# Queuing the ranking of a block's tokens in its last chunk's fifth turn instead of after its ninth

## The chip, the cores and the metric

The kernel runs on one core of one Trainium2 chip. The metric is the device time of one execution in microseconds (us). Before the change it is 3864.69 us, the median of four runs that lie between 3862.81 and 3876.28 us.

## The reference, cut to what matters

The program computes two layers, each of two halves. The change lies in the last quarter: a recurrence over 512 time steps, whose output goes token by token through a mixture of experts.

```python
def step(h_prev, xw_t):                       # second recurrence, 512 steps, batch 8, width 256
    h_next = jnp.tanh(xw_t + h_prev @ Wh)
...
router_logits = jax.nn.sigmoid(x @ gate_w + gate_b)             # 16 experts
expert_values, expert_indices = jax.lax.top_k(router_logits, k=2)
expert_values = expert_values / jnp.sum(expert_values, axis=-1, keepdims=True)
...
expert_weighted = jnp.sum(expert_values[..., None] * selected, axis=2)
return x + _mlp(x, shared_wg, shared_wu, shared_wd) + expert_weighted
...
x = x + _L1_ffn_ref(_L1_cond2_ref(x, cond_1024, ...), ...)      # experts of the recurrence's output
```

The tokens that enter the experts are the recurrence's hidden states; `_mlp` is the shared expert.

## The kernel before, in words

Everything up to the second recurrence (attention, a first recurrence, routed heads, adapters, a second attention) takes the first 3.1 ms and is not touched. `rnn_moe` (printed below) then runs the recurrence and the experts side by side on one core.

**Steps and passes.** The main loop makes 512 passes, one for each time step t. A pass issues, in this order: the step itself (`rnn_step`: 16 small matmuls of L1538 into `pg`, one tanh on ScalarE at L1540, one transpose on VectorE at L1541 that writes `ring`, which the next step's matmuls read); what an earlier pass left for later (`consume`); one piece of ranking (`ranks`); one piece of collecting (`gathers`); and one piece of bulk work, from `chunks` if there is one, else from `big`. A pass with neither gets one filling matmul (L1958). PE, ScalarE and VectorE execute in exactly this written order. POOL and SP are ordered by the scheduler.

**Chunks and blocks.** 16 steps (128 tokens) make a chunk. 32 chunks are cut into blocks of 9, 9, 9 and 5. When a chunk's 16 steps are done, `Experts.chunk` is queued. It takes nine turns, one in each of the following passes:

- turn 1: POOL copies the hidden states into `hT` (L1582); turn 2: nothing
- turn 3: router matmuls (L1594, L1595); their bias, sigmoid and the copy `hr` are left for the next pass
- turn 4: half of the shared expert (L1609); the maxima and their indices (`top`, `topi`, L1612, L1613) are left for the next pass
- turn 5: the other half (L1618); the gate `a` (L1622 to L1624) is left for the next pass
- turns 6 and 7: nothing; turns 8 and 9: `pd` (L1631, L1635), and the sum `acc` (L1639) left for the next pass

A turn that does nothing passes the place on to `big`.

**Ranks.** When a block's last chunk is through, `ranked(x)` is queued. `Experts.rank` turns the chosen experts into a row number for each token in a list that is sorted by expert and padded to tiles of 128 rows. That is 13 turns of small VectorE operations (L1653 to L1710) with three matmuls `pk` (L1677 to L1679) in the fifth turn. Then POOL scatters the rows of `hr` into DRAM with indirect DMAs (L1720), two for each chunk, in three turns for each pair. Each waits for the transpose of the step beside which it is issued (`paced`). Six idle turns follow, then the block's tiles are appended to `big`.

**Tiles.** A block has 33 tiles of 128 rows (25 in the last). `big` is a list worked off from the front, so the tiles of a block begin when those of the block before are done. The first five turns only load; then each tile takes three turns: two with `gate` (L1771) and a turn of the next rows (`turn`, L1761), one with `down` (L1787). POOL copies each tile's expert weights out of SBUF (L1751, L1752, two instructions) into one of four buffers, after the `down` that last used it. Outputs go to DRAM (L1792).

**Collecting.** When a block's tiles are done, POOL gathers their rows back with indirect DMAs (L1830), two for each chunk, and VectorE adds them (L1838).

After step 511 the same loop goes on without steps until all queues are empty. This part is called the drain here. It begins with the nine turns of the last chunk.

Of the kernel before, what the change touches and what calls it, by code (L numbers as in the profile page):

```python
# [1486 lines left out]
def rnn_project(K, M):  # L1487

    ahead = [chunk_x(K, M, n, "xp") for n in (1, 2)]
    for n in range(1, S // XB):  # L1490
        xc = ahead.pop(0)
        if n + 2 < S // XB:
            ahead.append(chunk_x(K, M, n + 2, "xp"))
        for m in range((n - 1) * 2 * M.NT // (S // XB - 1), n * 2 * M.NT // (S // XB - 1)):
            K.nc.sync.dma_start(out=M.xs[m // M.NT][m % M.NT * P : (m % M.NT + 1) * P, :], in_=M.zero)
        px = (M.psx, M.pxt)[n % 2].tile([P, D], F32, name="px", tag=("px", "xt")[n % 2])
        for k in range(2):
            K.nc.tensor.matmul(px, xc[:, k], M.wx[:, k, :], start=(k == 0), stop=(k == 1))
            if k == 1:
                M.later(lambda n=n, px=px: K.nc.vector.tensor_tensor(M.xw[:, n - 1, :], px, M.rbias, ALU.add))  # L1500
            yield 1


def expert_weights(K, M):

    src = M.experts.rearrange("(e p) n -> p e n", p=P)
    for e in range(16):
        K.nc.sync.dma_start(out=M.wgu[:, e], in_=src[:, e, 0 : 2 * D])
        K.nc.sync.dma_start(out=M.wdn[:, e], in_=src[:, e, 2 * D : 3 * D])
        yield 0  # L1510
# [335 lines left out]
def rnn_moe(K, out, start):  # L1846
# [3 lines left out]
    with ExitStack() as es:  # L1850
# [76 lines left out]
        big, ranks, chunks, gathers = [rnn_project(K, M), expert_weights(K, M)], [], [], []  # L1927

        def ranked(x):
            yield from x.rank()  # L1930
            for _ in range(6):
                yield 0
            big.append(tiled(x))

        def tiled(x):
            yield from x.tiles()
            gathers.append(x.collect())

        def chunk(x, c, ring):
            yield from x.chunk(c, ring)  # L1940
            if c == x.C - 1:
                ranks.append(ranked(x))

        M.left = True
        nb, at = -1, 0
        with K.tc.manual_schedule(engines={E.PE, E.Activation, E.DVE}):
            for t in range(S):
                if t % XB == 0:
                    if t == XB * sum(BLOCKS[: nb + 1]):
                        nb += 1  # L1950
                        block, at = Experts(K, M, nb), 0
                rnn_step(K, M, t)
                consume()
                advance(ranks)
                advance(gathers)
                idle = not (advance(chunks) or advance(big))
                if idle:
                    mm(M.pgu.tile([P, P], F32, name="fill", tag="gu"), K.ident, M.wx[:, 0, 0:P], start=True, stop=True)  # L1958
                for j in ((0, 1), (2,), (3,), ())[t % 4]:
                    if t // 4 * 4 + 4 < S:  # L1960
                        rnn_seed(K, M, t // 4 * 4 + 4, j)
                if t % XB == XB - 1:
                    chunks.append(chunk(block, at, M.ring))
                    at += 1
            while chunks or ranks or big or gathers:
                consume()
                M.left = bool(chunks or ranks or big)
                advance(ranks)
                advance(gathers)
                if advance(chunks) or advance(big):  # L1970
                    M.pace = M.last
            consume()
# [179 lines left out]
```

## Time and profile before

| what | us |
|---|---|
| median of four runs (3862.81, 3863.55, 3865.82, 3876.28) | 3864.69 |
| the profiled execution | 3875.72 |
| its span, first to last instruction | 3874.0 |
| first and last transpose of the recurrence (L1541, 512 of them) | 3099.5 and 3719.7 |
| the drain, from there to the end of the span | 154.3 |
| first VectorE instruction of the four ranks (L1653) | 3266.6, 3442.5, 3630.0, 3724.8 |
| scatters of the four blocks, first and last start (L1720) | 3281.3 to 3321.2, 3458.6 to 3498.0, 3646.1 to 3687.1, 3735.2 to 3757.3 |
| gathers of the four blocks, first and last start (L1830) | 3518.8 to 3597.4, 3721.6 to 3772.7, 3804.6 to 3841.4, 3855.0 to 3866.4 |

All times in the lower rows count from the span's start. The profiled execution is at the slow end of the four runs. In profile lines PE is the matmul engine, PEld its weight loads, DVE is VectorE, ACT is ScalarE, SPq is the queue of the engine that issues plain DMAs; a line ends with the idle time ahead of the instruction and what ended it.

### The profile page before, as it was taken

What the parts mean: (1) busy time and instruction counts of PE and PEld (TensorE: products, weight loads), DVE (VectorE), ACT (ScalarE), POOL (GpSimd) and SP (SyncE); (2) the same over time, 40 slices, a digit from 0 to 9 for tenths busy, and PEclk for the clock granted to TensorE, in tenths of its full rate; (3) what the DMA queues carried; (4) which work ended last, traced back from release to release, by engine and by line L of the source; (5) the groups of instructions that cost most, each with busy time, mean ns of one, the idle gap of its engine ahead of it and who ended that gap; (6) DMA issues with size and microseconds to landing.
All of it is one profiled execution on the core that took longest, in us unless ns stands there. A gap on an engine that the chain in (4) does not pass through costs nothing.

```text
span 3874.0 us, 146239 instructions
## 1 busy us (share of the span) xinstructions
PE 3442.5 (89%) x62442; PEld 2311.2 (60%) x62442; DVE 2373.8 (61%) x8871; ACT 1618.0 (42%) x5695; POOL 663.2 (17%) x1479
## 2 busy tenths in 40 slices
PE   8999888878888888699999999999999899999986
PEld 5533455555556556466656666666666666666665
DVE  4488667767777677466767666666766533243444
ACT  3111255555555555355644444444444322233333
POOL 1000000000000000000023223222323111233366
PEclk9899999999999999899999999999999999899998
DMA  3022100000000000200000000000000060122245
GB/s 111 27 83 69 32 21 16 22 21 16 5 5 5 5 4 10 75 26 26 1 3 2 1 1 2 1 2 2 1 7 1 6 210 18 59 74 81 86 128 158
DMA packets 102924, 137.91 MB, mean 36 GB/s; under 512 B 12336, under 2 KB 84048, under 8 KB 102144
## 3 DMA queue, kind: packets, MB, share of 16 engines
q1 hardware_dynamic: 88416, 89.03, 7.4%
q0 software_dynamic: 11040, 34.29, 2.7%
q8 instruction: 490, 8.03, 0.9%
q10 hardware_dynamic: 2816, 5.24, 0.4%
q14 instruction: 162, 1.33, 0.1%
HBM read 86.44 MB, written 43.25 MB: 33 GB/s over the span
## 4 chain that ended last, share of the span: by engine, by line
PE 65%; ACT 14%; DVE 12%; issue 5%; POOL 2%; DMA 1%; ACTq 0%; SPq 0%; POOLq 0%; DVEq 0%
PE pgf L678 5%; PE pg L1538 5%; PE pe L1245 4%; PE pt L1288 3%; PE po L1303 3%; DVE G L684 3%; PE pp L1205 3%; PE U L489 3%; PE pk L468 3%; PE px L1324 3%; PE pg L1771 3%; ACT th L694 3%; ACT so L685 2%; ACT left L685 2%; ACT right L685 2%
## 5 line engine op out<-in xcount | busy, mean ns | idle before, releaser
L678 PE MATMUL pgf<-wh,ring 128*16 128x64 f32 x8176 | 215.2, 223 | 201.9 <-DVE ring L695 199.5
L1541 DVE STREAM_TRANSPOSE ring<-h 128x64 f32<-128x64 f32 x512 | 125.6, 245 | 393.3 <-ACT h L1540 380.3
L678 PEld LDWEIGHTS pgf<-wh,ring 128*16 128x16 f32 x8176 | 127.4, 99 | 393.5 <-DVE ring L695 393.3
L1265 ACT ACTIVATE sm<-sm,nm 128x388 f32<-128x388 f32 (+3 forms) x512 | 283.5, 555 | 182.9 <-DVE nm L1261 182.6
L685 ACT ACTIVATE sf<-G 128x16 f32<-128x16 f32 x512 | 110.4, 216 | 462.8 <-DVE G L684 462.8
L1540 ACT ACTIVATE h<-pg 128x64 f32<-128x64 f32 x512 | 114.8, 224 | 448.9 <-PE pg L1538 397.1
L1538 PE MATMUL pg<-down,ring 128*16 128x64 f32 x8176 | 234.2, 226 | 36.6 <-DVE ring L1541 29.1
L1290 ACT COPY eT<-pt 128x512 f32<-128x512 f32 (+1 forms) x192 | 105.6, 550 | 357.0 <-PE pt L1288 356.7
L1205 PE MATMUL pp<-hn,wqkv 128*128 128x512 f32 x512 | 241.4, 615 | 0.8 <-DVE xT L932 0.8
L1288 PE MATMUL pt<-ident,sm 128*128 128x128 f32 x1280 | 192.6, 283 | 55.5 <-DVE sm L1271 41.5
L1272 POOL COPY pme<-sm 128x4 f32<-128x4 f32 x512 | 119.8, 235 | 645.3 <-DVE sm L1271 641.4
L1288 PEld LDWEIGHTS pt<-ident,sm 128*128 128x128 f32 x1280 | 148.2, 143 | 137.4 <-issue 81.7
L678 PE MATMUL pgo<-wh,ring 128*16 128x64 f32 x8176 | 216.5, 219 | 14.4 <-issue 14.0
L678 PE MATMUL pgg<-wh,ring 128*16 128x64 f32 x8176 | 212.5, 219 | 4.7 <-issue 4.4
L684 DVE STREAM_TRANSPOSE G<-pgf 128x64 f32<-128x64 f32 x512 | 127.6, 249 | 137.5 <-PE pgf L678 131.8
L637 POOL COPY xc<-xT 128x128 f32<-128x128 f32 x64 | 17.1, 296 | 1136.8 <-DVE xT L552 1025.2
L678 PE MATMUL pgi<-wh,ring 128*16 128x64 f32 x8176 | 209.6, 219 | 1.3 <-issue 1.3
L1538 PEld LDWEIGHTS pg<-down,ring 128*16 128x16 f32 x8176 | 144.9, 100 | 88.1 <-DVE ring L1541 67.5
L1261 DVE CUSTOM_DVE_ANT_0 sm<-pe,mask 128x260 f32<-128x260 f32 (+2 forms) x384 | 141.8, 425 | 89.1 <-PE pe L1245 88.9
L1771 PE MATMUL pg<-xT,w 128*128 128x128 f32 x992 | 168.6, 297 | 22.5 <-POOL w L1751 16.4
L1271 DVE TENSOR_SCALAR sm<-sm,rc 128x388 f32<-128x388 f32 (+3 forms) x512 | 176.1, 387 | 9.1
L695 DVE TENSOR_TENSOR ring<-so,th 128x16 f32<-128x16 f32 x512 | 90.0, 176 | 147.3 <-ACT th L694 147.3
(534 smaller groups left out, 8230.6 us busy)
## 6 DMA issues: line engine op xcount, KB each, us to landing
cb<-order POOLq DMA_DIRECT2D x32, 512.0 KB
x<-xs SPq DMA_DIRECT2D x124, 128.0 KB
ys<-y SPq DMA_DIRECT2D x124, 128.0 KB
xs<-zero SPq DMA_DIRECT2D x66, 128.0 KB
w<-in_ada_w_dram SPq DMA_DIRECT2D x16, 512.0 KB
w<-in_moh_w_dram SPq DMA_DIRECT2D x32, 195.0 KB
xres<-xp SPq DMA_DIRECT2D x32, 128.0 KB
xc<-xres SPq DMA_DIRECT2D x32, 128.0 KB
```

What stands on the lines that cost most here:

```text
L678: mm(dst[32 * j : 32 * j + B * (now + 1)], hp, w, start=False, stop=(k == 1), skip_group_check=True)
L684: nc.vector.transpose(G.rearrange("p k b -> p (k b)"), banks[n][0])
L685: nc.scalar.activation(to, G[:, :, B * now : B * now + B], f)
L1205: mm(pp, T.wqkv[:, k, 0 : 2048].rearrange("p (i g h n) -> p i g h n", i=2, g=4, h=2)[:, i, g, h], self.hn[b][:, k, :], start=(k == 0), sto ...
L1245: mm(pe[a][:, 0 : w - lo], q[r, h, at], k[r, h, lo:w], start=(h == 0), stop=(h == 1))
L1261: nc.vector.tensor_tensor_reduce(out=sm[a][:, lo:w], in0=pe[a][:, 0 : w - lo], in1=T.mask[:, S - n + lo : 4 + S], scale=-1.0 / 8.0, scalar ...
L1265: nc.scalar.activation(sm[a][:, 0:w], sm[a][:, 0:w], AF.Exp, bias=nm[:, a : a + 1], scale=-1.0, accum_out=su[:, a : a + 1])
L1271: nc.vector.tensor_scalar(sm[a][:, 0:w], sm[a][:, 0:w], rc[:, a : a + 1], None, ALU.mult)
L1288: nc.tensor.transpose(pt[:, at, :], sm[i * m + a][:, 4 + j * P : 4 + (j + 1) * P], K.ident)
L1538: mm(pg[32 * j : 32 * j + B * (now + 1)], hp, M.wh[:, k, 64 * j : 64 * j + 64], start=False, stop=(k == 1), skip_group_check=True)
L1541: M.pace = nc.vector.transpose(M.ring[:, B + 64 * at : B + 64 * at + 64], h)
L1771: mm(pg, W[m][:, k * D + g * P : k * D + (g + 1) * P], X[m][:, k, :], start=(k == 0), stop=(k == 1))
```

## The change

`ranked(x)` of a block is queued inside the last chunk's fifth turn, not after its ninth. The maxima and indices that the ranking reads are issued in that same pass, by its `consume`; the ranking's first piece follows in the next pass. Nothing else is edited.

```diff
         def chunk(x, c, ring):
-            yield from x.chunk(c, ring)
-            if c == x.C - 1:
-                ranks.append(ranked(x))
+            for n, used in enumerate(x.chunk(c, ring)):
+                if n == 4 and c == x.C - 1:
+                    ranks.append(ranked(x))
+                yield used
```

`rank` itself begins with `ti` copied from `topi` (L1653), and needs of the last chunk only `topi`, `top` and `hr`, all of which exist after its fourth turn.

## The prediction

> **What bounds the kernel now.** The page's busy line and its chain by engine come first: PE is busy for 89% of the span and carries 65% of the chain that ended last; POOL looks idle.
>
> ```profile
> PE 3442.5 (89%) x62442; PEld 2311.2 (60%) x62442; DVE 2373.8 (61%) x8871; ACT 1618.0 (42%) x5695; POOL 663.2 (17%) x1479
> ...
> PE 65%; ACT 14%; DVE 12%; issue 5%; POOL 2%; DMA 1%; ACTq 0%; SPq 0%; POOLq 0%; DVEq 0%
> ```
>
> That is an average over stages. The change touches only 3260 us to the end, so I read the view of waits for 3100 to 3700 us: who waited for whom, total us, times, longest.
>
> ```profile
> DVE ring L1541 <- ACT h L1540: 366.6, 454, 2.1
> ACT h L1540 <- PE pg L1538: 363.6, 438, 2.3
> POOL w L1751 <- PE py L1787: 154.4, 51, 12.1
> ```
>
> The recurrence is a ring of PE, ACT and DVE, each waiting for the one before: 512 transposes from 3099.5 to 3719.7, 620.2 us, 1.21 us a step. Its 512 steps must run whatever is queued beside them. Their pace from the timeline: steps 209 to 297 (tiles beside them, no indirect DMA) take 98.95/88 = 1.124 us each, the last three (fills beside them) 1.05. So what matters is (a) how long single steps are, (b) what work is left for the drain after step 511, which takes 3874.0 - 3719.7 = 154.3 us.
>
> **What the change moves.** The ranking is queued in the chunk's fifth turn, so its first piece falls in the sixth pass of the next chunk's time instead of the eleventh: five passes earlier. Before, the first DVE instruction of three ranks (L1653) starts at 3266.6, 3442.5 and 3630.0 us, which by counting transposes is beside steps 154, 298 and 442. They become 149, 293, 437. No instruction is added or removed; VectorE's some 30 small operations, the three `pk` matmuls and the scatters keep their number.
>
> *How far that carries* is counted from the code, pass by pass. Thirteen turns of ranking lead to the first scatter (step 167, as the trace has it: 3281.3 us), 26 more passes to the last, then idle turns.
>
> - Block 0: tiles are appended in pass 200, now 195. A chunk holds the place in its turns 3 to 5, 8 and 9, so tiles begin in pass 201, now 197: four earlier.
> - Blocks 1 and 2 do not wait for their ranks. Block 1's tiles are ready in pass 344 but the place is free in 353; block 2's in 488 but free in 510. The place becomes free when block 0's 107 turns have found room between chunks; its run starts four passes earlier but meets one chunk more, so it ends in 351, and block 1's in 508. Gain for block 2: **two passes**, not five.
> - The last block's rank starts five turns earlier in the drain, but its tiles wait for block 2's, some 60 turns later. Nothing.
>
> *What two passes are worth.* Block 2's first five turns only load. Before, they fall in passes 510 to 513 and 517, partly beside the last chunk; now in 508 to 512. Passes with nothing for PE are filled: 91 fills in the recurrence before, 91 after (two fewer ahead of block 0's tiles, five at block 1's start both ways, four instead of two at the end). In the drain 185 passes carry PE work before and 185 after; only empty passes, which issue nothing, fall from 31 to 29. So PE's work on either side of step 511 is the same, and two passes x 1.05 us = 2.1 us is not simply saved: they turn into two more fills.
>
> *The recurrence.* What makes steps long beside the ranks is the scatters. In block 2's, steps 455 to 482 take 3645.54 to 3687.26 = 41.7 us for 27 steps; at 1.125 that were 30.4; 18 scatters cost 11.3, **0.63 us each**. The timeline shows one:
>
> ```profile
> 3459.42 0.24 DVE L1541 STREAM_TRANSPOSE ring<-h 128x64 f32<-128x64 f32 x1 [0.94 <-ACT h L1540]
> ...
> 3459.72 0.42 PE L1538 MATMUL pg<-down,ring 128*16 128x64 f32 x16
> ...
> 3459.95 0.97 POOL L1720 DMA_INDIRECT xs<-hr,row  x1 [0.41 <-DVE ring L1541]
> ...
> 3461.51 0.23 ACT L1540 ACTIVATE h<-pg 128x64 f32<-128x64 f32 x1 [2.12 <-PE pt L1761]
> ...
> 3461.77 0.24 DVE L1541 STREAM_TRANSPOSE ring<-h 128x64 f32<-128x64 f32 x1 [2.10 <-ACT h L1540]
> ```
>
> PE's matmuls end at 3460.14, yet ACT starts at 3461.51, 0.6 us after the indirect DMA's issue ends: this step takes 2.35 us. The Trainium skill (SBUF — State Buffer, "SBUF: two separate sides") says that of the engines only VectorE and GpSimd contend, and PE and ACT wait for nobody; by that rule no scatter would cost anything here. The trace speaks against it, and I go by the row.
>
> All 54 scatters and 18 gathers of blocks 0 to 2 stay beside steps, five passes earlier: 0 change, between -1.9 and +1.9 if three meet steps differently (3 x 0.63). On POOL's queue they pass one chunk's `hT` copy per block (one behind them in place of two), and the idle list of PE for the stage shows no wait of L1594 on `hT`; worth nothing. The ranks' DVE work now shares passes with the chunk's gate `a` (two operations of 0.29 us) instead of a tile's `ea` (0.25 to 0.29): +0.3 at most in each of three blocks, against `pk` waits of the same size. I take 0. On SP the loads of `x` move with the tiles; L1761 waits for no DMA in this stage, so nothing is lost there.
>
> *The start of the drain.* Here an order changes. Before, POOL has the last chunk's `hT` first, then block 1's gathers; now two gathers stand ahead of `hT`.
>
> ```profile
> 3719.98 0.73 POOL L1582 COPY hT<-ring 128x128 f32<-128x128 f32 x2 [1.01 <-DVE ring L1541]
> 3720.43 0.51 PE L1594 MATMUL ph<-wr,hT 128*128 128x144 f32 x2 [0.66 <-POOL hT L1582]
> 3721.61 1.00 POOL L1830 DMA_INDIRECT yg<-ys,row  x1 [0.90 <-issue]
> 3722.91 0.97 POOL L1830 DMA_INDIRECT yg<-ys,row  x1 [0.30 <-issue]
> 3723.27 0.67 PE L1631 MATMUL pd<-wd,a 128*128 128x256 f32 x2 [0.89 <-DVE a L1624]
> ...
> 3729.15 0.61 POOL L1751 COPY w<-xT 128x512 f32 x1 [1.47 <-PE py L1787]
> ```
>
> The first gather waits for the last store of block 1's outputs (landed 3718.87 + 1.51 = 3720.38 in the chain of waits), which now comes two steps, 2.1 us, sooner: near step 510. The second is paced by step 511. Term by term:
>
> - one gather now beside a step: +0.6 (the 0.63 above; bounds 0 and 1.05, the excess of single slow steps in the gather stage)
> - `hT` behind a gather: +1.0 (bounds 0 and 2 x 1.28, the spacing of the gathers above). Queued behind `ph` on PE is all of the drain.
> - two transposes of block 2's first tile now stand ahead of `ph`: -0.4 (0.38 us, L1761)
> - PE's 0.89 wait for the gate is covered by `turn` and `gate` work that now stands ahead of `pd`: -0.9
> - the last rank's `pk` stands three gates earlier and may wait for its DVE chain: +0.4 (0.3 in the trace before; bounds 0 and 1)
> - the gathers done early free POOL, but it then waits longer for `down` (the 1.47 above): 0. After that POOL is the bound to 3758 us, with the same number of copies, scatters and gathers ahead of its ninth copy, less waits of 0.54 and 0.22: -0.8
>
> Sum: +0.6 + 1.0 - 0.4 - 0.9 + 0.4 - 0.8 = **-0.1 us**. On the profiled execution's own 3875.72 that is 3875.6. That execution lies 11.0 above the median of the four runs, so I carry the difference over: 3864.69 - 0.1, **3864.6 us**.
>
> **Clock.** The table by stretch shows granted clocks of 0.88 and 0.85 at block 0's scatters:
>
> ```profile
> 3250.00:3300.00 50.00, 46.19 (x835) 31.90 (x828) 18.60 (x88) 10.48 (x47) 14.05 (x22) 0.88 0.09 29
> 3300.00:3350.00 50.00, 44.17 (x766) 30.22 (x766) 12.64 (x59) 11.27 (x51) 11.20 (x14) 0.85 0.17 54
> ```
>
> Price: block 0's scatter steps take 42.6 us where 27 x 1.05 + 18 x 0.63 = 39.7 is due (+2.9), and the 14 steps after them 17.7 for 15.0 (+2.7): **5.6 us** for the pair of dips. The skill (TensorE: Matmul & The Clock Gate, "What's actually happening") says that the gate watches free-running windows of 3413 ns and halves the clock after an idle one; by it, dips would follow the windows' phase and not the edit, and the four runs' spread of 13.5 us would be the same after.
>
> **Rivals.**
>
> 1. *The two passes are kept and POOL is the bound from the drain's start*: -2.1 and two gathers off its queue, -2 x 1.28, gives -4.7: 3860.0. For it: POOL is saturated from 3735. Against: its 1.47 wait for PE just before.
> 2. *Five passes are gained*, as if tiles waited for ranks: -5 x 1.05 = -5.3: 3859.4. Against: the slack of 9 and 22 passes in blocks 1 and 2.
> 3. *The `hT` order decides* (slower): POOL's two gathers both go ahead, `hT` is 2.6 late, one step is 1.05 longer, and nothing covers it: +3.6: 3868.3. It decides once `hT` is later than the 1.3 us that two transposes and the gate wait cover. With one more pair of clock dips, at the four fills and the wait that now end the recurrence, +9.2: 3873.9; past 3876.3 only with a second pair.
> 4. *A pair of dips goes*: -5.6: 3859.1, with rival 1 3854.4.
>
> **How the numbers follow.** Forecast 60% (3861 to 3868); rival 1 10%, rival 2 5%, rival 3 12% (5 of them with dips), rival 4 5%, further off on the slow side 5, on the fast side 3. What a measurement of this kernel tells from no change is about 0.3%, 11.6 us: under 3853.1 faster, over 3876.3 slower. Faster 0.05 (3 far off, 2 of rival 4), slower 0.08 (5 far off, 3 of rival 3 with a second pair of dips), same 0.87. The range runs from rival 4 with 1 to rival 3 with dips: 3854 to 3874.
>
> **What would show it.** L1653 beside steps 149, 293, 437. Block 2's first transposes after step 511, as before; fills beside steps 508 to 511. The recurrence 620 +- 4 us, the drain 154 +- 3. Scatters still some 0.6 us each. Two gathers ahead of the last `hT`. I am wrong if the drain is over 4 us shorter or a stage of scatters is over 5 us longer than before at full clock.

## The result, and the profile after

The changed kernel takes 3876.56 us (median of 46 runs, 3866.14 to 3883.45). The kernel before, run in turn with it on the same chip, takes 3869.53 us (73 runs, 3860.29 to 3884.91). The ratio is 1.0018, 95% interval 1.0014 to 1.0023: **slower by 7.0 us**. That is inside the 0.3% that the prediction called no change, but it is no accident of the measurement, and the forecast of -0.1 us with its place in the middle of the range was wrong. The four runs shown before were a low sample (3864.69 against 3869.53). Laid on them, +7.0 would give 3871.7, inside the range; measured, the time lies above it.

The page's busy line and chain by engine, after the change, tell nothing of it:

```profile
PE 3440.4 (89%) x62442; PEld 2311.1 (60%) x62442; DVE 2373.6 (61%) x8871; ACT 1616.8 (42%) x5695; POOL 661.3 (17%) x1479
...
PE 65%; ACT 14%; DVE 12%; issue 5%; POOL 2%; DMA 1%; ACTq 0%; SPq 0%; POOLq 0%; DVEq 0%
```

The same holds for the view of waits for 3100 to 3700 us after the change (who waited for whom, total us, times, longest):

```profile
ACT h L1540 <- PE pg L1538: 380.0, 435, 21.4
DVE ring L1541 <- ACT h L1540: 364.6, 460, 2.9
POOL w L1751 <- PE py L1787: 155.0, 55, 8.7
```

They are the same three waits as before, of about the same size, and the longest of 21.4 us is that of the first step for work ahead of the recurrence, whose start differs from one execution to the next: its first transpose starts at 3104.26 us where it was 3099.46, though nothing before it was edited. So I compare stages from their own starts only.

| stage, us | before | after |
|---|---|---|
| profiled execution, its span | 3875.72, 3874.0 | 3877.89, 3876.1 |
| recurrence, first to last transpose (L1541) | 620.21 | 617.33 |
| steps 149 to 209 / 293 to 353 | 81.26 / 79.24 | 79.36 / 81.54 |
| steps 353 to 437 / 437 to 511 | 108.08 / 95.60 | 104.15 / 95.83 |
| drain, last transpose to end | 154.28 | 154.54 |
| last `hT` copies (L1582), after the last transpose | +0.3 | +2.9 |
| last router matmul (L1594), after it | +0.8 | +3.4 |
| first `down` of the drain (L1787), after it | +8.7 | +11.1 |

In this pair of profiles the recurrence is not slower. At the start of the drain everything is 2.4 to 2.6 us late. POOL's timeline of the changed kernel there (start, duration, operation, in brackets the idle time before it and what ended it):

```profile
3722.21 1.00 POOL L1830 DMA_INDIRECT yg<-ys,row  x1 [3.37 <-DVE ring L1541]
3723.51 0.97 POOL L1830 DMA_INDIRECT yg<-ys,row  x1 [0.30 <-issue]
3724.50 0.72 POOL L1582 COPY hT<-ring 128x128 f32<-128x128 f32 x2
...
3733.45 0.61 POOL L1751 COPY w<-xT 128x512 f32 x1 [4.58 <-PE py L1787]
```

And PE's timeline of the same kernel:

```profile
3721.52 0.38 PE L1761 MATMUL pt<-ident,x 128*128 128x128 f32 x2
3724.95 0.51 PE L1594 MATMUL ph<-wr,hT 128*128 128x144 f32 x2 [3.04 <-POOL hT L1582]
...
3728.41 1.06 PE L1631 MATMUL pd<-wd,a 128*128 128x256 f32 x2
```

The last transpose starts at 3721.59. POOL could then copy `hT`, but its queue holds two gathers first, so the copies start at 3724.50. PE executes in written order: it stands still for 3.04 us ahead of the router, though later work of tiles is there. POOL's own next weight copy then waits 4.58 us for `down`, where it waited 1.47. The chain of waits of the changed kernel says why the first gather was not beside step 510:

```profile
3718.70 2.37 DMA ys<-y
...
3722.21 1.00 POOL yg L1830
```

Block 1's last store is issued at 3718.70, 2.9 us ahead of the last transpose where it was 0.8: the two steps are there. But its last part lands at 3721.07, and the gather starts 1.14 us after that. The bracket of the gather's line names the last transpose, since that ended later (3721.83). But over the six profiles of kernels that have two gathers ahead of the copies, the gather starts between 0.60 and 1.20 us after the last transpose and always 1.13 or 1.14 us after the store has landed: it is the store that sets its start.

A last view, busy time by stretch, shows the granted clock (a share of full speed; a stretch at half clock is called a dip) after PE's wait in the changed kernel (columns: stretch, its length, busy us of PE, PEld, DVE, ACT and POOL with counts, granted clock, DMA share, GB/s):

```profile
3721.90:3724.90 3.00, 0.00 (x1) 0.00 (x0) 0.00 (x0) 0.37 (x1) 2.38 (x4) 1.00 0.31 87
...
3726.30:3729.70 3.40, 3.40 (x16) 3.22 (x16) 2.49 (x16) 1.13 (x4) 1.96 (x3) 0.53 0.42 117
3729.70:3733.00 3.30, 3.20 (x26) 2.75 (x24) 2.18 (x14) 0.75 (x3) 0.00 (x0) 1.00 0.24 70
```

PE is empty for 3 us, and about a microsecond after it has started again it runs at 0.53 for a stretch of 3.4 us; so `pd` takes 1.06 us instead of 0.67. Before, the same place was at 1.00. The Trainium skill (TensorE: Matmul & The Clock Gate, "What's actually happening") tells of such a gate: half clock after an idle window of 3413 ns. The dip's 3.4 us agree with the length of that window; the idle stretch of 3.0 us is shorter than one, so an idle window is not what this row shows.

### The profile page after: what moved, and what is told of

The parts are those of the page before. It is cut to its first block, busy times and chain, and to the rows that moved or that the text cites. A ratio compares the mean times of both kernels' runs of the same rounds, so it can differ in the third digit from the quotient of the medians.

```text
span 3876.1 us, 146241 instructions
## 1 busy us (share of the span) xinstructions
PE 3440.4 (89%) x62442; PEld 2311.1 (60%) x62442; DVE 2373.6 (61%) x8871; ACT 1616.8 (42%) x5695; POOL 661.3 (17%) x1479
## 4 chain that ended last, share of the span: by engine, by line
PE 65%; ACT 14%; DVE 12%; issue 5%; POOL 2%; DMA 1%; ACTq 0%; SPq 0%; POOLq 0%; DVEq 0%
PE pgf L678 5%; PE pg L1538 5%; PE pe L1245 4%; PE pt L1288 3%; PE po L1303 3%; DVE G L684 3%; PE pp L1205 3%; PE U L489 3%; PE pk L468 3%; PE px L1324 3%; PE pg L1771 3%; ACT th L694 3%; ACT so L685 2%; ACT left L685 2%; ACT right L685 2%
## 5 line engine op out<-in xcount | busy, mean ns | idle before, releaser
L1541 DVE STREAM_TRANSPOSE ring<-h 128x64 f32<-128x64 f32 x512 | 125.5, 245 | 390.2 <-ACT h L1540 377.9
L1245 PE MATMUL pe<-kt,qt 32*128 32x132 f32 (+3 forms) x2048 | 179.9, 466 | 0.0
```

Source lines behind the costliest of these rows:

```text
L1245: mm(pe[a][:, 0 : w - lo], q[r, h, at], k[r, h, lo:w], start=(h == 0), stop=(h == 1))
L1541: M.pace = nc.vector.transpose(M.ring[:, B + 64 * at : B + 64 * at + 64], h)
```

## The experiments

Three theories went into them. **H** (rival 3 of the prediction): the last `hT` copies stand behind two gathers on POOL, and PE's wait for them is the loss. **S**: the earlier scatters meet the steps worse. **C**: not the wait, but the clock dips that happen to come with it. Two kinds of chip came up: the kernel before takes 3869.83 and 3866.52 us on two of them, 3821.95 and 3823.97 on two others. So all comparisons are ratios to the kernel before on the same chip.

### One block at a time

The edit, here for block 0 (the others have 1, 2 or 3 in its place, or both 1 and 2):

```diff
+            early = x.nb == 0
             for n, used in enumerate(x.chunk(c, ring)):
-                if n == 4 and c == x.C - 1:
+                if n == 4 and c == x.C - 1 and early:
                     ranks.append(ranked(x))
                 yield used
+            if c == x.C - 1 and not early:
+                ranks.append(ranked(x))
```

> Only block 0's ranks begin five passes early; block 2's tiles then still begin two passes early (508). Theory H (two gathers stand ahead of the last chunk's state copies on POOL at the drain's start): slower by 2.5 to 3.5 us, PE waits some 3 us at L1594 after step 511, and the first weight copy of the drain comes 11.9 us after the last transpose in place of 9.5. Theory S (scatters of each block meet the steps at a worse phase): 0 to +2 us from block 0's scatters, no more in the drain. Theory C (more half-clock time while fills run at block 0): slower by 3 us or more, all of it between steps 149 and 209.

> Only block 1's ranks begin early; its tiles still wait for block 0's (pass 353), so nothing but the place of 18 scatters and 18 ranking passes moves. Theory S: slower by 2 to 2.5 us, all of it between steps 293 and 353, as in the profile of the full change (81.5 us against 79.2). Theories H and C: within 0.5 us of before.

> Only block 2's ranks begin early; its tiles still begin in pass 510. Theory S: 0 to +1 us, between steps 437 and 509 (93.7 us against 93.5 in the two profiles). Theories H and C: within 0.5 us of before, the drain's start with the state copies first, as before.

> Only the last block's ranks begin early, in the drain; the recurrence is as before. All theories: within 1 us of before. If its matmuls for the ranks make PE wait for VectorE at the drain's start, up to 1 us slower.

Before takes 3821.95 us on this chip. Block 0 alone: 3821.22, ratio 0.9999 (0.9988 to 1.0009). Block 1: 3816.84, 0.9994 (0.9984 to 1.0005). Block 2: 3821.03, 0.9999 (0.9990 to 1.0008). Block 3: 3824.06, 1.0002 (0.9993 to 1.0011). No ratio stands out. The order on POOL does: with block 0 alone the copies come behind two gathers, 3.5 us after the last transpose; with each of the others they are ahead of all gathers. So block 0's rank alone makes the new order, as the pass count of the prediction implies, since it alone moves the tiles. On this chip, H's loss of 2.5 to 3.5 us did not show in the time, though the profile has the wait (3.62 us ahead of the router) and the longest drain of all (158.12 us). Something came back earlier: steps 149 to 209 take 66.0 us in the four profiles with block 0 early on chips of the short kind, without a dip, and 67.3 to 69.5 in the four others there, three of them with dips.

> Blocks 1 and 2 early, block 0 and the last one as before. Theory S where the steps are held back by indirect DMAs: 2 to 3 us slower than before; where they are not: within 0.5 us. Theory H: 0 in both, since block 2's tiles begin in pass 510 and the state copies stand first.

> Block 0 early alone, which has the same order of gathers ahead of the state copies, once more. Theory H: 1.0008 to 1.0016, so that the first figure was at the edge of its interval (to 1.0009). If the wait costs nothing by itself: 0.9995 to 1.0003 again.

On the chips with the longer time: blocks 1 and 2 together 3868.81, 0.9999 (0.9989 to 1.0010). No loss shows from 36 scatters five passes earlier, but the 2 to 3 us of theory S (1.0005 to 1.0008) lie inside the interval. Its stage is longer: steps 293 to 353 take 80.3 to 81.9 us in all six profiles with block 1 early on these chips, and 79.2 to 79.9 in the four without, 1.4 us apart in the mean. So theory S is not excluded for an amount of that size. Block 0 alone again 3871.06, 1.0010 (1.0001 to 1.0020): slower, beside the changed kernel's 1.0020 in the same session.

> The full change once more. Before ran at 3869.5 us where the change was first timed, and at 3822 us where the four parts were; there the stages with indirect DMAs took 10 to 14 us less each. If indirect DMAs hold the steps back here (before near 3870): ratio 1.0014 to 1.0023, as recorded, with block 1's stage (steps 293 to 353) 2 us longer than before's. If they do not (before near 3822): theory S gives less than 1.0005, theory H (state copies behind two gathers) 1.0005 to 1.001.

> The full change, on whatever chip comes. Where before takes near 3870 us: ratio 1.0014 to 1.0018 as twice before. Where it takes near 3822 (indirect DMAs do not hold the steps back): theory H alone gives 3 to 6 us slower, 1.0008 to 1.0016; if only block 0's figure (0.9999 with the same wait) is right, something in the recurrence gives back as much and the ratio is 0.9995 to 1.0005.

The change itself: 3874.59, 1.0014 (1.0003 to 1.0024), and 3873.90, 1.0020 (1.0011 to 1.0028). With the first result that is 5.4, 7.0 and 7.7 us (ratio times the time before) in three sessions. The 2 us that were expected between steps 293 and 353 were 1.4 and 0.3 there, beside the profiles of before from the same chips.

### The copies first, all else as changed

The scheduler decides POOL's order, so the changed kernel got an order that it must keep: gathers of the drain stand behind the last `hT` copies.

```diff
         self.K.tc.add_manual_dep(dma.ins, self.M.pace.ins.name, info, reason="one at a time")
+        if self.M.drain:
+            self.K.tc.add_manual_dep(dma.ins, self.M.copied.ins.name, info, reason="behind the copies")
...
-            nc.gpsimd.tensor_copy(
+            M.copied = nc.gpsimd.tensor_copy(
...
-                advance(gathers)
+                if t < 509:
+                    advance(gathers)
...
+            passes, M.drain = 0, True
...
-                advance(gathers)
+                passes += 1
+                if passes > 1:
+                    advance(gathers)
```

> The full change, but block 1's gathers are held until the last chunk's state copies are issued on POOL. Theory H: 2.5 to 3.5 us below the full change, the first weight copy of the drain 9.5 us after the last transpose and not 11.9. Theory S alone: the same as the full change.

> Copies first once more, for a narrower interval: ratio to before 0.9990 to 1.0005; theory H asks for 5 to 8 us below the full change where before is near 3870, and 3 to 6 where it is near 3822.

> Copies first beside the full change on one chip. Theory H: 3 to 7 us below the full change, ratio to before 0.9990 to 1.0002. If the wait costs nothing where steps are not held back: the same as the full change.

Measured in three sessions: 3867.56, 0.9998 (0.9988 to 1.0008); 3822.10, 0.9996 (0.9988 to 1.0005); 3869.29, 1.0005 (0.9997 to 1.0014). In the first and third the changed kernel on the same chip was at 1.0014 and 1.0020. POOL and then PE in the first of them:

```profile
3717.62 0.73 POOL L1584 COPY hT<-ring 128x128 f32<-128x128 f32 x2 [3.05 <-DVE ring L1541]
3718.71 1.00 POOL L1832 DMA_INDIRECT yg<-ys,row  x1 [0.36 <-POOL hT L1584]
...
3726.38 0.68 POOL L1753 COPY w<-xT 128x512 f32 x1 [2.87 <-PE py L1789]
```

```profile
3718.07 0.51 PE L1596 MATMUL ph<-wr,hT 128*128 128x144 f32 x2 [0.45 <-POOL hT L1584]
...
3722.99 0.45 PE L1680 MATMUL pk<-half,ones 128*128 128x80 f32 x2 [0.83 <-DVE half L1672]
```

PE's wait for the copies falls from 3.04 to 0.45 us, and its first `down` comes 8.4 us after the last transpose, as before the change (8.7). The two passes stay gained, the ranks stay early, the scatters stay where the change put them: so what goes here hangs on the order on POOL. It is 7.0 and 4.6 us, from medians of the two kernels on one chip, where 2.5 to 3.5 and 3 to 7 were expected. The three ratios also agree with the other half of the prediction's sum: with the delay gone, no gain shows either. The granted clock in the stretch behind it, same columns as above:

```profile
3719.00:3722.40 3.40, 3.13 (x23) 2.54 (x21) 2.63 (x17) 1.35 (x5) 2.64 (x3) 1.00 0.45 137
```

### The wait without the change

The kernel before, with its last copies put behind the first gather of block 1 (and the other gathers behind the copies):

```diff
-            nc.gpsimd.tensor_copy(
+            copied = nc.gpsimd.tensor_copy(
...
+            if self.first + c == S // XB - 1:
+                K.tc.add_manual_dep(copied.ins, M.gathered.ins.name, info, reason="behind a gather")
+                M.copied = copied
...
-                    self.paced(
-                        nc.gpsimd.indirect_dma_start(
+                    M.gathered = nc.gpsimd.indirect_dma_start(
...
+                    self.paced(M.gathered)
```

> The kernel before, with one thing changed: block 1's first gather stands ahead of the last chunk's state copies on POOL. The gather waits for block 1's last store, so the copies come some 2.9 us after the last transpose, as in the full change, and not 0.3. Theory H: slower than before by 4 to 7 us without any rank moved. If the loss of the full change has another cause: within 1 us of before.

3829.39 us against 3823.97: 1.0016 (1.0008 to 1.0025). Its timeline of POOL and of PE:

```profile
3673.29 1.00 POOL L1835 DMA_INDIRECT yg<-ys,row  x1 [2.74 <-issue]
3676.13 0.73 POOL L1584 COPY hT<-ring 128x128 f32<-128x128 f32 x2 [1.84 <-DMA yg<-ys,row]
```

```profile
3676.57 0.85 PE L1600 MATMUL ph<-wr,hT 128*128 128x144 f32 x2 [5.21 <-POOL hT L1584]
```

The dose is larger than I meant: the copies waited for the gather to land (1.84), so PE stood for 5.21 us, not 3.0, and the second gather starts 5.9 us after the last transpose instead of 3.2. A late copy, with no rank, tile or scatter queued earlier, makes the kernel slower by 5.4 us.

### The late copies, with PE's wait covered

The changed kernel, with three more empty turns in the last chunk ahead of its router, so that PE gets tile work there; the last rank is queued three turns later to keep its place behind the experts.

```diff
         yield 0
         yield 0
+        if self.first + c == S // XB - 1:
+            for _ in range(3):
+                yield 0
...
-                if n == 4 and c == x.C - 1:
+                if n == (4 + 3 if x.nb == 3 else 4) and c == x.C - 1:
```

> The full change with three more empty turns in the last chunk ahead of its router, so that PE has block 2's first gates to do while the state copies wait behind the gathers. The copies are as late as in the full change. If PE's uncovered wait is the cost: 4 to 7 us below the full change, near before. If what follows the copies (the last block's ranks and scatters) is the cost: as the full change or up to 3 us slower.

3823.23 us against 3823.97: 1.0001 (0.9992 to 1.0009). Its timeline of POOL and of PE:

```profile
3667.31 1.00 POOL L1833 DMA_INDIRECT yg<-ys,row  x1 [3.34 <-DVE ring L1541]
3668.61 0.98 POOL L1833 DMA_INDIRECT yg<-ys,row  x1 [0.30 <-issue]
3669.59 0.73 POOL L1582 COPY hT<-ring 128x128 f32<-128x128 f32 x2
...
3676.85 0.61 POOL L1754 COPY w<-xT 128x512 f32 x1 [2.87 <-PE py L1790]
```

```profile
3667.76 0.61 PE L1774 MATMUL pg<-xT,w 128*128 128x128 f32 x4
...
3670.04 0.51 PE L1597 MATMUL ph<-wr,hT 128*128 128x144 f32 x2 [0.77 <-POOL hT L1582]
```

POOL's order is that of the changed kernel, and the copies are as late (+2.9), but `gate` work runs in the gap, PE waits 0.77 us, and the first `down` is at +9.4. Before is not the best measure here, since block 0's early rank may give something back on this kind of chip. The copies first on the same chip are: 3822.10 us, 1.1 us less, with intervals that overlap widely. So the late copies themselves cost nothing measurable; PE's uncovered wait is what remains in the kernels that lose. The same edit with two empty turns and the copies first was the control:

> Copies first, and two more empty turns ahead of the last chunk's router: both covers at once. If the wait of 0.66 us at the drain's start and the one for the gate (0.9) are all that is left to cover: 0 to 2 us below copies first, so 1 to 3 us below before. A version that beats both kernels, if there is one on this path.

3822.96 us, 0.9999 (0.9990 to 1.0007): the turns alone neither gain nor cost, and the 1 to 3 us below before do not show. These kernels ran on a chip of the short kind, where the changed kernel itself was not timed and where block 0 alone had shown no loss; so this pair shows the direction, and the size of the loss is from the other chips.

### The kernel before once more

> The kernel before, for a profile from the same chip as the other three of this call. Its time is that of before here; its stages are the measure for theirs. If before is near 3822 here, its 72 indirect DMAs beside steps cost under 0.15 us each; near 3870, 0.6 us each.

> The kernel before, for a profile from the same chip: its recurrence and drain are the measure for the other three. Where before takes near 3822, a recurrence of 570 to 573 us and a drain of 151 to 155.

Two more profiled executions of before (3876.38 and 3869.73 us), for the spread: recurrence 619.53 and 614.75, drain 154.69 and 151.61, first `down` 8.7 after the last transpose in both. Single profiles thus differ by 5 us in a stage with the same program. Over all profiles, the six with late copies and an open wait have a mean drain of 156.0 us, the other twelve 152.6: **+3.4 us**, with overlap (154.12 the shortest of the six, 154.87 the longest of the twelve).

## Why the prediction was wrong, step by step

- **What the change moves: right.** The first instructions of three ranks (L1653) stand beside steps 149, 293 and 437; block 2's first transposes follow step 511; fills stand beside 508 to 511. Two passes, not five.
- **Scatters 0 +- 1.9: not contradicted, but not shown either.** Blocks 1 and 2 early give 0.9999 with an interval of 0.0010 either way. Steps 149 to 209 moved both ways with their dips; steps 293 to 353 are some 1.4 us longer with block 1 early, while the three profiles of before differ there by 0.7.
- **Recurrence 620 +- 4, drain 154 +- 3: both held in the profile, and say little.** 617.33 and 154.54. The loss of 7 us could not have been read from this pair of executions; the medians and the place of `hT` showed it.
- **"one gather now beside a step: +0.6" and "`hT` behind a gather: +1.0": the step that failed.** I put the first gather near step 510, with only the second in the way of the copies. Both started after the last transpose, at +0.6 and +1.9, so no gather stood beside a step, and `hT` came at +2.9: 2.6 later where the sum has 1.0, and at the upper bound of 2.56. Two things were missed. First, I read 3720.38 as the landing of block 1's last store; that piece of the chain ends where PE's wait for `hT` ends. The trace has the store's last part landing at 3720.57, 1.70 us after its issue, and POOL starts such a gather 1.0 to 1.1 us after the landing, which I left out. With both, the first gather comes within 0.2 us of the last transpose's start even with two steps gained (-0.80 - 2.1 + 1.70 + 1.0 to 1.1), and the copies behind both gathers. Second, the store took 2.37 us instead of 1.70 after the change: fifteen of its sixteen parts had landed after 1.69, the last came late. That made it +0.6.
- **"PE's 0.89 wait for the gate is covered: -0.9", "`pk` +0.4": right in kind, and no help.** The wait ahead of `pd` is gone, and `pk` waits 0.83 for its chain in the kernel with the copies first (0.30 before). From the router to the first `down` it is 7.91 us before, 7.64 with the copies first, and 7.75, 8.62 and 8.61 in three profiles of the changed kernel. What I counted against the delay of `hT` lies behind it, not beside it: only the two transposes stand ahead of the router, and PE's wait was 3.04 us long with them already done.
- **Rival 3, given 12%, came true in its mechanism, its place and its 2.6 us.** Its 1.05 for one longer step did not come. Its price of +3.6 was too small for the ratios (5.4 to 7.7 us), and +9.2 with a pair of dips too large. The first `down` is 2.4, 3.5 and 3.4 us later than before in three profiles of the changed kernel. In all six profiles with a long wait of PE at the drain's start a dip comes with it (3.4 us in two of the three of the changed kernel, 6.8 in the third), and in none of the twelve others; my sum had put dips there at nothing. By the mean drains, 3.4 us of the loss are found.
- **Theory C, as far as the record goes.** Every run lists its mean granted clock. Within a session a run is 2.0 to 2.5 us shorter for each 0.001 of clock more. A straight line through the runs of two kernels, with a step between them, gives the difference at equal clock: the changed kernel is 5.3 and 4.7 us slower than before on the two chips of the long kind, the copies first 2.2 and 2.3 (standard errors 0.8 to 1.0). So dips on the whole do not make the loss: by this estimate 3.1 and 2.4 us hang on the order, about the wait's own length, and the rest of the medians' 7.0 and 4.6 between these two kernels goes with the clock. How much of that the wait itself brings on is open, since every kernel that waits longer also has the dip.
- **Open: some 2 us that stay with the copies first.** At equal clock they stand against before on both chips of the long kind, and not on the short kind (0.1, standard error 0.8). Steps 293 to 353 may hold most of them; no run tests that. Block 0 alone lost nothing on one chip (interval up to 1.0009) and 1.0010 on another; what steps 149 to 209 gave back on the first is a likely reason, not a tested one.

No version here is faster than the kernel before beyond its interval. PE executes as many matmuls as before (62442), and the two passes gained in the recurrence come back as fills, as forecast.

## What to carry to other kernels

When a change brings an operation's input forward, ask for the queue it waits in: if a scheduler orders that queue, work that becomes ready a little sooner can pass ahead of a small copy on which an engine in written order stands. Read the start of the waiting operation in the trace, not the landing of what it waits for. And a cover counts only if it is issued ahead of the wait; cover behind it is another saving.

## What the runs showed of the hardware

Two things were not expected. The first: the same program takes 3870 and 3867 us on two chips and 3822 and 3824 on two others. The difference is in the stages where indirect DMAs of POOL stand beside steps: 353 to 437 takes 104.5 to 108.1 us (three profiles of before on chips of the long kind) against 94.8 to 95.1 (the kernels with one of blocks 1 to 3 early, on a chip of the short kind), while steps 209 to 293, without them, take 94.40 on both. One step beside a scatter, in the changed kernel on a chip of the long kind:

```profile
3460.99 0.44 PE L1538 MATMUL pg<-down,ring 128*24 128x64 f32 x13
3461.14 0.97 POOL L1720 DMA_INDIRECT xs<-hr,row  x1 [1.58 <-DVE a L1623]
3462.45 0.22 ACT L1540 ACTIVATE h<-pg 128x64 f32<-128x64 f32 x1 [1.70 <-PE py L1787]
```

And one in the kernel with block 3 alone, on a chip of the short kind:

```profile
3612.13 0.41 PE L1538 MATMUL pg<-down,ring 128*8 128x64 f32 x16
...
3612.52 0.97 POOL L1720 DMA_INDIRECT xs<-hr,row  x1 [0.30 <-DVE ea L1781]
3612.68 0.23 ACT L1540 ACTIVATE h<-pg 128x64 f32<-128x64 f32 x1 [0.80 <-PE pg L1538]
```

In the first, ScalarE starts 1.02 us after the matmuls end, 0.34 after POOL's instruction is over; the `py` that its bracket names ended 0.39 us before. In the second it starts 0.14 us after the matmuls, while POOL's instruction runs. 72 of them (54 scatters, 18 gathers) at the prediction's 0.63 us are 45 us, by this estimate about the whole difference of 43 to 48 us between the chips. So the rule that the prediction set aside (the Trainium skill, SBUF — State Buffer, "SBUF: two separate sides": PE and ScalarE wait for nobody) agrees with the row of one kind of chip and not with that of the other. The same section has VectorE and GpSimd block each other, so that "no scatter would cost anything" goes further than the page. Whether it is SBUF that ScalarE waits for, and why the chips differ, no run here shows.

The second: half clock also comes where PE is never idle for long. The stretch 3250 to 3300 us of the changed kernel, with PE busy for 44.92 of 50 us and never idle for more than 1.23 us at a time, has a granted clock of 0.93, and the one after it 0.87; before, it was 0.88 and 0.85.

```profile
3250.00:3300.00 50.00, 44.92 (x842) 30.55 (x842) 18.63 (x88) 10.21 (x46) 13.82 (x21) 0.93 0.10 32
3300.00:3350.00 50.00, 44.48 (x795) 31.14 (x794) 12.89 (x61) 11.77 (x53) 11.32 (x16) 0.87 0.17 55
```
